# New figures in the account that orders TensorE's queue: weight loads behind a wait, transposes, projections, sums

## The chip, the core and the metric

The kernel runs on one core of one Trainium2 chip. The metric is the device time of one execution in microseconds, the median of three timed runs. The profile comes from one further execution of the same kernel. TensorE multiplies matrices and transposes, VectorE and ScalarE read its results out of eight banks, GpSimd works on data in the on-chip memory, and SyncE issues most of the DMAs.

## The reference, cut to what matters

One decoder layer is computed for 4 batches of 1,024 rows with 256 features: causal self-attention with 16 heads of 16, then cross-attention to 77 context rows under a mask, then a gated feed-forward part with 768 hidden features. Each part works on the layer-normalised rows and is added to the residual.

```python
x = x + attn(layernorm(x))      # scores = (gt*Qt K^T + (1-gt)*Q (M K)^T) * 16**-0.5, causal,
                                # softmax, times V, times Wo.T, plus bo
x = x + xattn(layernorm(x), ctx, ctx, mask)   # q Wq, k Wk, v Wv, softmax of 16 heads, times Wo
x = x + ffn(layernorm(x))       # h = silu(x wg.T / 127) * (x wu.T / 127);  h wd.T / 127
```

## The kernel before

The rows are cut into chunks of 512: two chunks n = 0, 1 for each of the four batches b. A chunk passes five generators, each of which emits its instructions piece by piece.

- `project` (two streams, one for each n) loads a chunk's rows, takes their statistics, normalises and transposes them, and makes q, k and v. A projection of q or k ends in `spread`: ScalarE writes the upper part `hi` (L782), VectorE the rest `lo` (L785, L787), and SyncE issues DMAs (L791) that lay both out by heads.
- `maxima` multiplies q with k in row blocks (L925, masks L933) and lets VectorE take each row's maximum `mt` (L938). After every second group of heads, `shift` transposes the maxima (L800) and leaves them as `ms` (L804).
- `attend` multiplies k with q (L998), adds the shift to the product on TensorE (L1004, masks L1011), lets ScalarE take the exponential `es` (L1017), and sums with the values (`weigh`, L1041). `quotients` transposes the sums back (L735) and divides; `out_proj` transposes (L197) and multiplies with the output weights (L769).
- `cross_attention` does the like for the 77 context rows (L1172 and L1180 for the maxima, L1226 for the scores, L1239 for the sums, L1146 for a mask).
- `ffn` normalises, transposes, multiplies with gate and up (`hidden`, L1296; ScalarE L1303 and L1308, VectorE L1304 and L1306, GpSimd L1309), and with the down weights (L1331, added to the rows at L1336).

Three further streams load and transpose the feed-forward weights, and one prepares the cross-attention weights.

The order of TensorE's queue is not written out; `weave` works it out while the program is built. Each stream offers its next piece: `piece(pe, use, at, free, mode, **take)`. `pe` is its length on TensorE, `use` a list of engines and lengths that come after it, `at` the time from which its data is expected, `take` the banks and buffers it needs. The mode is "rows" where the array's upper and lower halves work side by side (score products), "cols" where four strips of columns do (the sums), otherwise "whole". `weave` keeps the time at which TensorE's queue ends, the expected busy spans of ScalarE, VectorE, GpSimd and the DMAs, and the time at which each bank and buffer comes free. At every step it computes the start t of each offered piece, adds an offset from the table `LATES` (one row for a stream, one entry for each chunk of it), and takes the first in the list of streams whose sum is within 0.01 us of the least. A change of mode adds `SWITCH`, 0.11 us.

Where the account expects TensorE to be idle for more than 1.3 us and a bank is free, it fills in dummies: `stirred` issues int((idle - 0.7) / 0.235) matmuls (L93) ahead of the piece.

From the first moment until the second group of the first maxima, the weave's order holds for TensorE and VectorE. After that it holds for TensorE alone; the other engines' queues are ordered by the scheduler of the framework. The queues of all engines run in their order. The eight banks are shared: a "single" piece takes one, a "pair" two neighbouring ones.

```python
with tc.manual_schedule(engines={ENG.PE, ENG.DVE}):
    weave(*streams, until="begun")
tc.no_sync_barrier()
with tc.manual_schedule(engines={ENG.PE}):
    weave(*streams)
```

Of the kernel before, what the change touches and what calls it, by code (L numbers as in the profile page):

```python
# [27 lines left out]
def tile_decoder_layer(  # L28
# [126 lines left out]
    w4 = ctx.enter_context(tc.tile_pool(name="w4", bufs=6))  # L155
# [298 lines left out]
    LATE = 0.2  # L454
# [57 lines left out]
    def weave(*streams, until=None):  # L512
        while True:
# [4 lines left out]
            for s in live:  # L518
                p = s.next
                if p["cond"] is not None and not p["cond"]():  # L520
                    continue
                t = max(
                    tensor["end"], p["at"], *(slots[k].when(c) for k, c in p["take"].items()), 0.0
                )
                if p["pe"] and p["mode"] != tensor["mode"]:
                    t += SWITCH
                if p["use"] and p["take"]:

                    eng, us = p["use"][0]
                    t = max(t, busy[eng].start(t + p["pe"], us) - p["pe"] - 1.0)  # L530
                if t < 1.0e8:
                    can.append((t + (s.lates[s.chunk] if s.lates else 0.0), t, s))
# [221 lines left out]
    def out_proj(st, nat, t_nat, w, xt):  # L754

        yield piece(
            1.1, use=[("ACT", 1.05)], at=st.done + LATE, pair=1, w4=1, free=[t_nat]
        )
# [4 lines left out]
        for half in range(2):  # L763
            yield piece(2.0, at=at, use=[("DVE", 0.7)], free=t_aT * half, single=1)
            t = single().rearrange("p (i d) -> p i d", d=D)
# [40 lines left out]

    SPREAD = [("ACT", 0.62), ("DVE", 0.77), ("DMA", 8.0)]

# [24 lines left out]
    def project(st, b, n):  # L833
# [4 lines left out]
        else:  # L838
# [7 lines left out]
            scales = row_scales(xn)  # L846
            yield piece(0.0, use=[("DVE", 1.5)], at=st.done)
            normal_rows(xn, *scales)
            flags.add(("normal", b, n))
            yield piece(  # L850
                1.1, use=[("ACT", 1.05)], at=st.done + LATE, pair=1, w4=1, free=t_xn
            )
# [4 lines left out]
        for c in range(NC):  # L857
# [8 lines left out]
            if c == 0:  # L866
                for half in range(2):
                    yield piece(
                        2.0, use=[("ACT", 0.7)], single=1,
                        cond=lambda: (b, n) != (0, 0) or ("normal", 0, 1) in flags,  # L870
# [25 lines left out]
    def maxima(st, b, n):  # L896

        nk = n + 1
        for g in range(NG):
# [52 lines left out]
            if g % 2:  # L952
                yield piece(
                    0.55, use=[("ACT", 0.6), ("DVE", 0.77)], at=st.done + 0.6, single=1, f2=1,
                    ms=1,
                )
                ms = shift(mpad, "ms")
                st.release("single")
                st.release("f2")
                shifts[b, n, c] = ms, st.done + LATE, st.got["ms"][0]  # L960

    def attend(st, b, n):
# [6 lines left out]
        for g in range(NG):  # L969
# [9 lines left out]
            for kb in range(nk):  # L979
# [49 lines left out]
                def weigh(g=g, kb=kb, ki=ki, lo=lo, w=w, both=both, vs=vs, acc=acc, toks=toks,  # L1029
                          ready=ready):  # L1030
                    last = kb == nk - 1
                    yield piece(
                        0.03 + w * 1.77e-3, at=ready, free=toks, mode="cols",
                        use=[("ACT", 0.6)] if last else [],
# [35 lines left out]
    def quotients(st, tail, nat, t_nat):  # L1070
        rest, toks, at, g = tail
        yield piece(
            0.55, use=[("DVE", 0.75)], at=at, single=1, free=toks,
            **({"w4": 1} if nat is None else {}),
# [40 lines left out]
    def cross_attention(st, b, n):  # L1115
# [11 lines left out]
        scales = row_scales(xt, keep[:, it])  # L1127
        yield piece(0.0, use=[("DVE", 1.5)], at=st.done)
        xn = normal_rows(xt, *scales, wide([P, QT, D], "xn"))
        for j in range(2):  # L1130
# [3 lines left out]
        yield piece(  # L1134
            1.1, use=[("ACT", 1.05)], at=st.done + LATE, pair=1, w4=1, free=t_xn
        )
# [4 lines left out]

        yield piece(0.55, use=[("ACT", 0.6), ("DVE", 0.6)], single=1, mx=1)
        t_mB = st.got["mx"]
# [47 lines left out]
        for j in range(2):  # L1191
# [4 lines left out]
        yield piece(  # L1196
            0.55, use=[("ACT", 0.6), ("DVE", 0.77)], at=st.done + 0.8, single=1, f2=1, mx=1
        )
# [7 lines left out]
        for g in range(NG):  # L1206
            both, toks = [], []
            for p in range(2):
# [23 lines left out]
            yield piece(  # L1232
                0.95, use=[("ACT", 0.6)], at=st.done + LATE, free=toks, single=1, f2=1,
                mode="cols",
# [18 lines left out]
    def ffn(st, b, n, xt=None, rest=()):  # L1253
# [12 lines left out]
        if st:  # L1266
            xt, _ = xs[b, n]
            nc.sync.dma_start(x_dram[b, n], xt)
        scales = row_scales(xt)
        yield piece(0.0, use=[("DVE", 1.5)], at=done())  # L1270
        xn = normal_rows(xt, *scales, wide([P, QT, D], "xn"))
        yield piece(
            1.1, use=[("ACT", 1.05), ("DVE", 1.25)], at=done(), pair=1, w4=2, free=t_xn
        )
# [9 lines left out]
        def hidden(hc):  # L1284

            for k in range(2):
                yield piece(
                    0.95, at=at, single=1, free=t_x if k and hc == NH - 1 else [],
                    use=[("DVE", 0.7), ("ACT", 0.5), ("POOL", 1.3)] if k else
                    [("ACT", 0.6), ("DVE", 0.75)],  # L1290
# [19 lines left out]
            if st:  # L1310
                st.release("single", st.done - 2.2)
                give(t_h[0], st.done)
# [3 lines left out]
        for hc in range(NH):  # L1316
            held.append((yield from hidden(hc)))
            while len(held) == 3 or (hc == NH - 1 and held):
                now, held = held[:2], held[2:]
                at_h = max(h[3] for h in now)  # L1320
                for half in range(2):
                    yield piece(
                        1.2, at=at_h, use=[("DVE", 0.72)], single=1,
                        free=[t for h in now for t in h[2]] if half else [],
# [22 lines left out]
    def every(part, lates, chunks=range(NQ)):  # L1347
# [11 lines left out]
        [0.0000, 0.0000, 0.0000, 0.0000, 0.0000, 0.0000, -0.1816, 0.0000],  # L1359
        [0.0000, 0.0000, 0.0000, 0.0000, 0.0000, 0.0098, 0.0000, 0.0000],  # L1360
        [0.1824, 0.0000, 0.0000, 0.0465, 0.0104, 0.0000, 0.0000, 0.0000],
        [0.0212, -0.2908, 0.0000, 0.0000],
        [0.0391, 0.1944, 0.3468, 0.0000],
        [-0.3083, 0.0025, 0.0000, 0.0000, 0.4000, 0.3194, 0.3283, 10.7883],
    )
# [69 lines left out]
```

## Time and profile before

| | |
|---|---|
| time, median of 3 runs | 1212.08 us (1208.81 to 1214.08) |
| the profiled execution | 1210.99 us, span 1209.2 us |
| granted TensorE clock, mean | 0.979 |
| TensorE matmul busy | 1115.3 us, 92%, 9,147 instructions |
| TensorE weight load busy | 685.7 us, 57% |
| VectorE busy | 730.2 us, 60% |
| ScalarE busy | 559.6 us, 46% |
| GpSimd busy | 131.0 us, 11% |
| dummies (L93) | 88 matmuls, 24.0 us |

The weight loads (PEld) run beside the matmuls (PE) and are not to be added to them. Idle time of an engine stands with the work that ended it: "PEld banks L925 <- DVE mt L938" means that a weight load of line 925 waited until VectorE's `mt` of line 938 was done; the numbers are the total in us, how often, and the longest. In a line of the timeline the first number is the start, the second the length, both in us. In a line of a stretch the numbers after its length are busy time and instructions of PE, PEld, DVE, ACT and POOL, then the granted clock, the DMA share and GB/s. The matmuls' ends are modelled, so two starts are the safer measure of what a piece costs.

### The profile page before, as it was taken

The numbers are of one execution on the slowest core, as the hardware profiler recorded it, in microseconds if no ns is written. First come the engines' busy times: TensorE is split into PE (matmuls) and PEld (weight loads), VectorE is DVE, ScalarE is ACT, GpSimd is POOL, SyncE is SP. The second block draws the span as 40 slices with busy tenths as digits, with TensorE's granted clock in tenths as the row PEclk, the third lists the DMA queues.
The fourth block names the chain that finished last, engine by engine and source line by source line (L and its number), as shares of the span: only waits on it lengthen the run. The fifth ranks groups of instructions, "written<-read, shape, count | busy, mean of one in ns | idle before, by whom it ended". The sixth has DMA issues, their size and how long they took to land.

```text
span 1209.2 us, 22461 instructions
## 1 busy us (share of the span) xinstructions
PE 1115.3 (92%) x9147; PEld 685.7 (57%) x9147; DVE 730.2 (60%) x1287; ACT 559.6 (46%) x785; POOL 131.0 (11%) x138
## 2 busy tenths in 40 slices
PE   6898889899999999989899998999899999998997
PEld 4544445455665557546646556455456755556675
DVE  5678863254678776245758558632678893317544
ACT  3143346644444554744343553565244456663332
POOL 4030100001100002101200002010000101003112
PEclk9899999999999999989999999999899999999999
DMA  6992233147254206345362433109931204202300
GB/s 125 132 176 68 63 50 78 22 68 105 50 74 68 37 18 88 75 66 70 71 86 23 68 60 52 64 18 126 119 52 21 41 10 98 25 19 40 49 35 21
DMA packets 65441, 76.48 MB, mean 63 GB/s; under 512 B 22450, under 2 KB 39398, under 8 KB 65331
## 3 DMA queue, kind: packets, MB, share of 16 engines
q1 hardware_dynamic: 64227, 74.62, 39.2%
q8 instruction: 74, 1.21, 0.5%
q10 hardware_dynamic: 1104, 0.35, 0.1%
q14 instruction: 36, 0.29, 0.1%
HBM read 15.28 MB, written 9.33 MB: 20 GB/s over the span
## 4 chain that ended last, share of the span: by engine, by line
PE 67%; DVE 11%; DMA 11%; ACT 6%; issue 2%; POOL 2%; SPq 1%; ACTq 0%; DVEq 0%; POOLq 0%
PE banks L1041 10%; PE banks L998 7%; PE banks L925 6%; PE banks L1296 6%; PE banks L819 5%; PE banks L1004 4%; DMA q<-lo 4%; PE banks L769 4%; DVE mt L938 4%; PE banks L1226 4%; PE banks L1331 3%; DMA k<-lo 3%; ACT es L1017 3%; PE banks L1239 3%; PE banks L197 2%
## 5 line engine op out<-in xcount | busy, mean ns | idle before, releaser
L1017 ACT ACTIVATE es<-banks 128x1024 f32<-128x1024 f32 (+3 forms) x384 | 298.6, 811 | 243.6 <-PE banks L1011 162.5
L938 DVE TENSOR_REDUCE mt<-banks 128x2 f32<-128x1024 f32 (+3 forms) x384 | 349.8, 952 | 99.8 <-PE banks L933 65.8
L925 PE MATMUL banks<-k,q 64*128 64x512 f32 (+3 forms) x768 | 163.6, 427 | 27.5 <-DVE mt L938 15.8
L998 PE MATMUL banks<-q,k 64*128 64x512 f32 (+3 forms) x768 | 161.9, 414 | 18.0 <-DVE mt L938 5.9
L1041 PE MATMUL banks<-es,vs 128*32 128x512 f32 (+3 forms) x1536 | 167.1, 508 | 1.9 <-ACT aS L730 0.8
L925 PEld LDWEIGHTS banks<-k,q 64*128 64x128 f32 x768 | 75.2, 187 | 115.6 <-DVE mt L938 42.6
L1004 PE MATMUL banks<-ms,sel 64*128 64x512 f32 (+3 forms) x768 | 136.6, 348 | 2.2 <-DVE ms L804 2.2
L998 PEld LDWEIGHTS banks<-q,k 64*128 64x128 f32 x768 | 74.4, 188 | 98.4 <-ACT es L1017 36.5
L1309 POOL TENSOR_TENSOR hT<-h,hT 128x512 fp32r<-128x512 f32 x48 | 61.6, 1284 | 365.7 <-ACT hT L1308 365.7
L740 DVE RECIPROCAL rd<-banks 128x16 f32<-128x16 f32 x64 | 15.9, 252 | 107.2 <-PE banks L735 91.3
L1228 ACT ACTIVATE es<-banks 77x1024 f32<-77x1024 f32 x64 | 63.1, 1018 | 34.5 <-PE banks L1226 34.1
L1004 PEld LDWEIGHTS banks<-ms,sel 64*128 64x128 f32 x768 | 75.5, 190 | 5.9 <-DVE ms L804 2.5
L933 PE MATMUL banks<-cm_qk,id 64*128 64x128 bf16 (+1 forms) x1024 | 67.9, 211 | 0.0
L1303 ACT ACTIVATE h<-banks 128x512 f32<-128x512 f32 x48 | 28.7, 597 | 84.8 <-PE banks L1296 76.2
L1011 PE MATMUL banks<-cm_kq,id 64*128 64x64 bf16 (+1 forms) x1024 | 67.6, 210 | 0.0
L178 POOL TENSOR_TENSOR rs<-ve,mhalf 128x4 f32<-128x4 f32 x24 | 24.3, 1015 | 376.3 <-DVE ve L176 376.2
L1331 PE MATMUL banks<-wdT,hT 128*128 128x256 f32 x384 | 56.5, 294 | 3.1 <-POOL hT L1309 1.7
L1041 PEld LDWEIGHTS banks<-es,vs 128*32 128x32 f32 x1536 | 32.0, 109 | 41.7 <-issue 24.2
L1331 PEld LDWEIGHTS banks<-wdT,hT 128*128 128x128 f32 x384 | 49.7, 192 | 9.8 <-issue 3.3
L1186 DVE TENSOR_REDUCE mx<-banks 128x8 f32<-128x616 f32 x64 | 47.4, 791 | 12.6 <-PE banks L1180 12.5
L1304 DVE SCALAR_TENSOR_TENSOR h<-h,banks 128x512 f32<-128x512 f32 x48 | 32.9, 686 | 31.2 <-ACT h L1303 30.4
L730 ACT COPY aS<-banks 128x512 f32<-128x512 f32 x64 | 37.4, 588 | 28.8 <-PE banks L1239 21.8
(182 smaller groups left out, 1627.3 us busy)
## 6 DMA issues: line engine op xcount, KB each, us to landing
q<-hi SPq DMA_DIRECT2D x128, 128.0 KB, 6.3
q<-lo SPq DMA_DIRECT2D x128, 128.0 KB, 6.8
k<-hi SPq DMA_DIRECT2D x64, 128.0 KB, 4.9
k<-lo SPq DMA_DIRECT2D x64, 128.0 KB, 6.3
xr<-in_x_dram SPq DMA_DIRECT2D x8, 512.0 KB, 5.0
x<-in_x_dram SPq DMA_DIRECT2D x8, 512.0 KB, 5.7
x_dram<-x SPq DMA_DIRECT2D x8, 512.0 KB, 5.5
out_dram<-x SPq DMA_DIRECT2D x8, 512.0 KB, 2.9
```

What stands on the lines that cost most here:

```text
L925: nc.tensor.matmul(t[:, j, :w], q[r, a, i * P : (i + 1) * P], k[r, a, :w], start=True, stop=True,)
L933: nc.tensor.matmul(t[:, j, w - P + 64 * half : w], id2[r, half], cm_qk[r, half, 64 * half :], start=False, stop=True, skip_group_check=True,)
L938: nc.vector.tensor_reduce(mt[:, i, :, p, kc], t[:, :, :w], AX.X, ALU.max)
L998: nc.tensor.matmul(t[:, j, lo:], k[r, a, ki * P : (ki + 1) * P], q[r, a, lo:], start=True, stop=False,)
L1004: nc.tensor.matmul(t[:, j, lo:], sel[r, hp, :], ms[r, lo:], start=False, stop=True)
L1011: nc.tensor.matmul(t[:, j, lo : lo + 64 * (half + 1)], id2[r, half], cm_kq[r, half, : 64 * (half + 1)], start=False, stop=True, skip_group ...
L1017: nc.scalar.activation(es[:, :, lo:], t[:, :, lo:], AF.Exp)
L1041: nc.tensor.matmul(acc[0][W * jj : W * (jj + 1), lo:], vs[:, ki, V1 * h : V1 * h + W], both[jj // 2][:, jj % 2, lo:], start=(kb == 0), sto ...
L1228: nc.scalar.activation(es[:S2], t[:S2], AF.Exp)
L1296: nc.tensor.matmul(t, w[:, c, hc * P : (hc + 1) * P], v[:, c, :], start=(m == 0), stop=(m == len(terms) - 1),)
L1309: nc.gpsimd.tensor_tensor(hs[:, 1, :], h, hs[:, 0, :].bitcast(F32), ALU.subtract)
L1331: nc.tensor.matmul(t[:, i, :], h[1][:, v, m0 : m0 + P], w[:, h[0], :], start=(m == 0), stop=(m == len(terms) - 1),)
```

## The change

The rule for the start of a piece is split. A piece in another mode than the one before starts when its data, its banks and TensorE's queue are there, plus 0.11 us, as before. A piece in the same mode now starts 0.11 us after its data and banks are there, or at the end of the queue if that is later; the first weights of such a piece count as loaded behind the wait. Beside it some lengths are changed: on TensorE those of transposes, output and value projections, sums with the values, and the feed-forward part's down products; on the other engines those of the normalising, the spread, the value copy, the division and one copy of the hidden rows. The tables `LATES` have new entries. No computation is added, taken away or changed.

```diff
-                t = max(
-                    tensor["end"], p["at"], *(slots[k].when(c) for k, c in p["take"].items()), 0.0
-                )
-                if p["pe"] and p["mode"] != tensor["mode"]:
-                    t += SWITCH
+                t = max(p["at"], *(slots[k].when(c) for k, c in p["take"].items()), 0.0)
+                if p["pe"]:
+
+                    if p["mode"] != tensor["mode"]:
+                        t = max(t, tensor["end"]) + SWITCH
+                    else:
+                        t = max(t + SWITCH, tensor["end"])
+                t = max(t, tensor["end"])
...
-            1.1, use=[("ACT", 1.05)], at=st.done + LATE, pair=1, w4=1, free=[t_nat]
+            0.92, use=[("ACT", 1.05)], at=st.done + LATE, pair=1, w4=1, free=[t_nat]
...
-            yield piece(2.0, at=at, use=[("DVE", 0.7)], free=t_aT * half, single=1)
+            yield piece(1.75, at=at, use=[("DVE", 0.7)], free=t_aT * half, single=1)
...
-    SPREAD = [("ACT", 0.62), ("DVE", 0.77), ("DMA", 8.0)]
+    SPREAD = [("ACT", 0.69), ("DVE", 0.77), ("DMA", 8.0)]
...
-            yield piece(0.0, use=[("DVE", 1.5)], at=st.done)
+            yield piece(0.0, use=[("DVE", 1.9)], at=st.done)
...
-                        2.0, use=[("ACT", 0.7)], single=1,
+                        1.75, use=[("ACT", 0.6)], single=1,
...
-                        0.03 + w * 1.77e-3, at=ready, free=toks, mode="cols",
+                        0.03 + w * 1.68e-3, at=ready, free=toks, mode="cols",
...
-            0.55, use=[("DVE", 0.75)], at=at, single=1, free=toks,
+            0.46, use=[("DVE", 0.72)], at=at, single=1, free=toks,
...
-                0.95, use=[("ACT", 0.6)], at=st.done + LATE, free=toks, single=1, f2=1,
+                0.9, use=[("ACT", 0.6)], at=st.done + LATE, free=toks, single=1, f2=1,
...
-                    use=[("DVE", 0.7), ("ACT", 0.5), ("POOL", 1.3)] if k else
+                    use=[("DVE", 0.7), ("ACT", 0.62), ("POOL", 1.3)] if k else
...
-                st.release("single", st.done - 2.2)
+                st.release("single", st.done - 2.32)
...
-                        1.2, at=at_h, use=[("DVE", 0.72)], single=1,
+                        1.0, at=at_h, use=[("DVE", 0.72)], single=1,
...
-        [0.0000, 0.0000, 0.0000, 0.0000, 0.0000, 0.0098, 0.0000, 0.0000],
-        [0.1824, 0.0000, 0.0000, 0.0465, 0.0104, 0.0000, 0.0000, 0.0000],
-        [0.0212, -0.2908, 0.0000, 0.0000],
-        [0.0391, 0.1944, 0.3468, 0.0000],
-        [-0.3083, 0.0025, 0.0000, 0.0000, 0.4000, 0.3194, 0.3283, 10.7883],
+        [0.0000, 0.0000, 0.0000, 0.0000, 0.0000, 0.0000, 0.0000, 0.0000],
+        [0.1824, -0.0676, 0.0000, 0.0000, 0.0136, 0.0000, 0.0000, 0.0759],
+        [0.0000, 0.0000, 0.0000, 0.0000],
+        [0.1069, 0.1944, 0.3468, 0.0000],
+        [0.0000, 0.0000, -0.5736, 0.0000, 0.0000, 0.4883, 0.5315, -4.4614],
```

The same pairs of figures (1.1 to 0.92, 0.55 to 0.46, 1.5 to 1.9) are set at the other places where eight or four transposes or the normalising are offered: in `project`, `maxima`, `cross_attention` and `ffn`.

## The prediction

> **What bounds the kernel now.** I read the page first (busy shares and the forty slices), then the waits of TensorE and of its weight loads, then the timeline where a wait is seen at close range, then the groups of VectorE and ScalarE, and last the stretches of 20 and 100 us. The profiled execution took 1210.99 us, with a span of 1209.2 us; the median of the three timed runs is 1212.08 us, 1.1 us above it.
>
> ```profile
> PE 1115.3 (92%) x9147; PEld 685.7 (57%) x9147; DVE 730.2 (60%) x1287; ACT 559.6 (46%) x785; POOL 131.0 (11%) x138
> ```
>
> TensorE has work in 92% of the span and holds 67% of the chain that ended last. No other engine is above 60%. So the time is the length of TensorE's own queue plus what it loses between its pieces: 94 us shown as idle, and more that the rows hide, because a matmul whose weights are loaded late is shown as busy. Nothing in the change alters how much TensorE computes. What it can move is the losses.
>
> ```profile
> PEld banks L925 <- DVE mt L938: 42.6, 74, 3.9
> PEld banks L998 <- ACT es L1017: 36.5, 60, 1.2
> PEld banks L925 <- ACT es L1017: 29.0, 46, 1.2
> PEld banks L998 <- DVE mt L938: 12.3, 14, 3.8
> ...
> PE banks L925 <- DVE mt L938: 15.8, 26, 3.7
> ...
> PE banks L925 <- ACT es L1017: 6.9, 16, 0.8
> ```
>
> The first four lines are weight loads of the two score products (maxima L925, attention L998) that waited for a bank: 74+60+46+14 = 194 times. The last two are the same waits of L925 where TensorE's matmul side also stood visibly idle; with the two rows of L998 in that view (5.9 us, 3 times, and 5.1 us, 12 times) that makes 26+16+3+12 = 57 times and 33.7 us. So about 137 loads waited without a visible hole: the bank came free while the previous matmul was still draining. The old account calls those free. The next rows show they are not.
>
> ```profile
> 1177.74 0.19 PEld L1296 LDWEIGHTS banks<-xl,wgT 128*128 128x128 f32 x1 [0.47 <-DVE xl L1279]
> 1177.74 0.50 PE L1296 MATMUL banks<-xl,wgT 128*128 128x512 f32 x1
> 1177.85 0.19 PEld L1296 LDWEIGHTS banks<-xh,wgT 128*128 128x128 f32 x1
> 1178.08 0.39 PE L1296 MATMUL banks<-xh,wgT 128*128 128x512 f32 x1
> 1178.31 0.39 PE L1296 MATMUL banks<-xl,wgT 128*128 128x512 f32 x1
> ```
>
> The matmul whose load waited is 0.50 us long, its equals 0.39: the load's 0.11 us is added, and the next starts 0.34 us later and not 0.23. That is the price, and it is `SWITCH`.
>
> **The change, part by part.** It adds and removes no instruction by itself and adds no wait; it changes figures with which the order of TensorE's queue is worked out, so every term is an effect of another order.
>
> *Loading behind a wait.* Now a piece in the same mode that becomes ready at time r starts at r + 0.11 or at the queue's end, whichever is later; before, at r or the end. The order can thus prefer a piece that is long ready to one that arrives just now. At stake: 137 × 0.11 = 15.1 us; nothing at the other end, since the ready alternative is often in another mode, whose switch costs the same 0.11. Between these I take one in three avoided, about 46 × 0.11 = 5 us gained. That share is my choice, no row gives it.
>
> [...]
>
> *Lengths on TensorE.* The account takes off: eight-transposes 39 × 0.18 = 7.0 us; four-transposes 96 × 0.09 = 8.6; output and value projections 48 × 0.25 = 12.0; weighing, 16 × (1,280 + 3,328) columns × 0.00009 = 6.6; cross weighing 32 × 0.05 = 1.6; the FFN's down sums 48 × 0.2 = 9.6. Together 45 us. The rows support each:
>
> ```profile
> 439.60 1.09 PE L197 MATMUL banks<-ident,nat 128*128 128x128 f32 x8
> 440.62 1.06 PE L1041 MATMUL banks<-es,vs 128*32 128x512 f32 x8
> 441.62 0.66 PE L735 MATMUL banks<-ident,aS 128*128 128x128 f32 x4
> 442.12 0.60 PE L800 MATMUL banks<-ident,mpad 128*128 128x128 f32 x4
> 442.55 3.62 PE L769 MATMUL banks<-xwo,xnT 128*128 128x256 f32 x16
> ```
>
> From start to start: 1.02 (0.92 + 0.11 switch), 1.00 (0.89 + 0.11), 0.50 and 0.43 (0.46), 3.55 for two halves (1.75 each; the next piece starts at 446.10). The 45 us are none of the chip's time. They only move where the account expects the other engines to be ready, nearer to the truth. I take 1 us gained; between 6 us gained and 6 lost, the size of one stall of the kind described next.
>
> *Lengths elsewhere.* Normalising 1.5 to 1.9, ScalarE's spread 0.62 to 0.69, the hidden cast 0.5 to 0.62, the value copy 0.7 to 0.6: the groups by form give 4 × 459 ns = 1.84 us (L186), 687 ns (L782 with a bias), 617 ns (L1308) and 587 ns (L887). Most of it shifts expectations as above. One cost is certain, at the tail. The weave fills an expected idle time with dummies, (idle - 0.7) / 0.235 of them.
>
> ```profile
> 1168.22 5.86 PEld L93 LDWEIGHTS banks<-sel,selB 128*128 128x128 f32 x26
> ...
> 1171.66 1.38 DVE L186 TENSOR_SCALAR xn<-x,mv,rs 128x256 f32<-128x256 f32 x4 [1.12 <-POOL rs L178]
> ...
> 1174.35 1.03 PE L197 MATMUL banks<-ident,xn 128*128 128x128 f32 x8
> ```
>
> VectorE is done at 1173.04, but the transposes start at 1174.35: the dummies already overrun. With 0.4 us more expected idle there are 1 or 2 more, each 5.86 / 26 = 0.225 us: 0.5 us lost on the path, no cover there.
>
> *Tables.* An offset matters only where another stream competes. The FFN's last entry (10.7883 to -4.4614) works when every other stream has ended, so it is worth nothing. The other 14 changed entries move a stream's pieces by up to 0.6 us against the others; their worth is in the next term.
>
> *Stalls that another order redeals.*
>
> ```profile
> 860.00:880.00 20.00, 13.64 (x76) 7.31 (x78) 10.06 (x23) 7.12 (x10) 2.48 (x3) 0.74 0.71 95
> ...
> 900.00:1000.00 100.00, 96.65 (x869) 59.90 (x870) 88.19 (x127) 44.76 (x60) 7.62 (x7) 1.00 0.19 26
> ```
>
> In the first line TensorE loses 6.4 us. VectorE's queue is not ordered by the weave there: a `lo` (L785) waited in it for ScalarE's `hi`, that one for a spread DMA, and the shift `ms` (L804) stood behind, for which L1004 waited 2.2 us. The stretches 120:160, 520:540 and 600:620 lose another 7.0, 3.2 and 4.0 us. [...] A redeal can lose it or make another: from 12 us gained to 10 lost; I take 2 gained, because the account's errors (a spread on ScalarE at 0.62 where 687 ns are measured) sit just in that chain.
>
> Sum: 5 + 1 - 0.5 + 2 = 7.5 us gained: 1210.99 - 7.5 = 1203.5 for a profiled execution, 1204.6 by the median.
>
> **The rivals.** *Nothing to be had.* The just-arrived piece gives way only to one in another mode, which pays the same 0.11, or to one waiting for the same bank. Then the 194 waits stay about 194 and only the tail term and small redeals remain: 1212. For it: VectorE and ScalarE release the banks at their own pace (1.22 us for a wide maximum); against: three streams and more usually have something ready.
>
> *Slower: the maxima starve VectorE.* The pieces that wait most are the maxima (74 + 46 of the 194), so the new rule pushes these back, and VectorE's reduction starts later by as much. Place: the stretches with VectorE near full, above all 900:1000, busy 88.2 of 100. A later chunk has 64 maxima pieces; 64 × 0.11 = 7 us of pushed-back reductions, against 11.8 us of slack. Once pushes pass 11.8 us in such a stretch (each set aside about twice), the shift comes late, attention's L1004 waits for `ms` as at 868, and TensorE runs dry: some 4 us and 2 us of half clock in perhaps two of the four batches, 12 us in all: 1224. For it: the margin is thin; against: where nothing else is ready the maximum still goes first.
>
> *The change does not do what it says.* The figures agree with the rows, so this is only that a truer account need not give a better order; it lies within the two rivals.
>
> **How the numbers follow.** Faster by order and account 0.42, own range 1192 to 1206; nothing to be had 0.22; slower by starving or a worse redeal 0.36, own range 1218 to 1230. The likeliest is 1204.6. Cases of both signs hold most of the chance, so the range runs from 1192 to 1226: gains at both bounds of the first two terms at one end, the starved batches at the other. The bound of 0.5% (6 us, about what a measurement of this kernel can tell from no change) is at 1206 and 1218; the chances are those of the cases.
>
> **What would show it.** Right: fewer than 160 waits of the weight loads in the four lines shown, TensorE's idle time below 90 us, the stretch around 860 without a half clock, and 27 or 28 dummies before the last transposes. Wrong: the four lines as before (no gain), or more PE waits on `ms` (L804) and VectorE's busy share in the fullest hundred us below 85% (starving), or a new stretch with a clock under 0.8.

## The result: slower by 0.7%, and the profile after

| | before | after |
|---|---|---|
| median of ten runs each, same chip visits | 1212.8 us (1208.15 to 1215.59) | 1220.85 us (1215.35 to 1226.38) |
| the profiled execution | 1210.99 us, span 1209.2 | 1220.41 us, span 1218.6 |
| granted TensorE clock, mean | 0.979 | 0.968 |
| TensorE idle (span less PE busy) | 93.9 us | 91.6 us |
| dummies (L93) | 88 | 112 |
| last reduction of the maxima (`mt`) ends at | 1000.3 us | 1040.1 us |

The ratio after to before is 1.0070, 95% interval 1.0045 to 1.0095: slower, where 1204.6 us was forecast. The lines of the changed kernel stand 3 higher (L925 is now L928, L998 L1001, L938 L941, L1017 L1020).

First the busy line of the page, then the group of L93 (the dummies), and then one line of the forty slices, the granted clock, after and before:

```profile
PE 1127.0 (92%) x9171; PEld 699.8 (57%) x9171; DVE 727.3 (60%) x1287; ACT 558.0 (46%) x785; POOL 131.0 (11%) x138
```

```profile
L93 PE MATMUL banks<-sel,selB 128*128 128x512 f32 x112 | 31.7, 431 | 6.4 <-DVE selB L590 6.4
```

```profile
PEclk9799999999899899998999998999989999999999
```

```profile
PEclk9899999999999999989999999999899999999999
```

Over the whole span TensorE is not idler than before. It is busy 11.7 us longer, with 24 instructions more; these are the dummies, 7.7 us of it. The rest, 4.0 us, is the same matmuls taking longer: six slices have an 8 or less in the clock's row, where three had before. A matmul at half clock shows as busy (before, the projection L819 x4 at 873.52, at a clock of 0.50, is 3.78 us long, where the one at 858.58 is 1.88), so this loss is found in no list of waits.

The waits of the weight loads, as the prediction read them (total us, times, longest us):

```profile
PEld banks L928 <- DVE mt L941: 47.0, 69, 3.6
PEld banks L1001 <- ACT es L1020: 45.9, 70, 1.4
PEld banks L928 <- ACT es L1020: 36.6, 55, 1.6
...
PEld banks L1001 <- DVE mt L941: 12.1, 14, 2.3
```

69 + 70 + 55 + 14 = 208, where there were 194. With the 57 that also left the matmul side idle taken off, 151 waited without a visible hole, where 137 had. The rule that charges 0.11 us for a load behind a wait has not made such loads rarer. The matmul side:

```profile
PE banks L928 <- DVE mt L941: 20.3, 24, 3.2
PE banks L928 <- ACT es L1020: 8.5, 18, 1.4
PE banks L329 <- DMA wk_n<-in_L_attn_Wk_dram: 8.1, 1, 8.1
PE banks L93 <- DVE selB L590: 6.4, 1, 6.4
```

The wait of L928 for `mt` grew from 15.8 to 20.3 us at about the same number, that for `selB` at the start from 2.4 to 6.4 (five dummies, which need `selB`, now go ahead of the second chunk's transposes). Other holes shrank by as much.

Where the time goes is found by laying the two traces side by side at equal amounts of TensorE work done (an estimate, as each matmul counts with what its kind usually takes). At about 926 us the changed kernel is some 1 us ahead; at about 1148 us it is some 10 us behind. The net loss arises in that stretch. Two lines from the stretches of 100 us after, and the second of them before:

```profile
900.00:1000.00 100.00, 92.10 (x845) 56.50 (x846) 71.88 (x115) 43.95 (x61) 5.85 (x5) 0.97 0.23 42
1000.00:1100.00 100.00, 97.32 (x873) 53.76 (x871) 40.24 (x66) 63.28 (x84) 1.86 (x2) 1.00 0.18 28
```

```profile
1000.00:1100.00 100.00, 99.44 (x837) 60.05 (x838) 32.27 (x77) 62.20 (x84) 7.66 (x7) 1.00 0.23 43
```

Before, the first of these had TensorE at 96.65 and VectorE at 88.19; now VectorE is at 71.88 and the maxima it has not done come 40 us later. Over these 200 us TensorE is idle for 10.6 us, where it was for 3.9. By then the fifth feed-forward chunk (b = 2, n = 0), which before lasted until 1008 us beside those maxima, is used up: it ended at 909 us. The stretch of the prediction's starved batch is the right one. That TensorE lacks the chunk's work there is a reading of these lines and is not shown.

A stall at close range, from the timeline (start, length; in brackets the idle time before it and what ended it):

```profile
408.62 1.02 POOL L178 TENSOR_TENSOR rs<-ve,mhalf 128x4 f32<-128x4 f32 x1 [42.37 <-DVE ve L176]
...
409.95 1.38 DVE L186 TENSOR_SCALAR xn<-x,mv,rs 128x256 f32<-128x256 f32 x4 [1.41 <-POOL rs L180]
...
411.24 3.02 DVE L941 TENSOR_REDUCE mt<-banks 128x2 f32<-128x1024 f32 x4
...
412.52 0.33 PE L928 MATMUL banks<-k,q 64*128 64x128 f32 x2 [3.21 <-DVE mt L941]
```

VectorE's queue reaches a normalising whose `rs` GpSimd has not yet made. VectorE stands 1.41 us, the normalising itself takes 1.38 us more, the reductions behind it are late, they hold the banks, and TensorE stands 3.21 us. The weave had not put the normalising there: in this part VectorE's queue is ordered by the framework. The half clock that follows (L772 x16 in 6.34 us, where it takes 3.6) lasts 6.8 us.

### The profile page after: what moved, and what is told of

It reads as the page before. It is cut to its first block, busy times and chain, and to the rows that moved or that the text cites. A ratio compares the mean times of both kernels' runs of the same rounds, so it can differ in the third digit from the quotient of the medians.

```text
span 1218.6 us, 22516 instructions
## 1 busy us (share of the span) xinstructions
PE 1127.0 (92%) x9171; PEld 699.8 (57%) x9171; DVE 727.3 (60%) x1287; ACT 558.0 (46%) x785; POOL 131.0 (11%) x138
## 4 chain that ended last, share of the span: by engine, by line
PE 70%; DVE 13%; ACT 6%; DMA 4%; issue 4%; POOL 2%; SPq 1%; ACTq 0%; DVEq 0%; POOLq 0%
PE banks L1044 11%; PE banks L928 7%; PE banks L1001 7%; PE banks L822 6%; PE banks L1299 5%; DVE mt L941 5%; PE banks L772 5%; PE banks L1007 4%; PE banks L1229 3%; PE banks L1334 3%; ACT es L1020 3%; PE banks L197 2%; PE banks L738 2%; PE banks L1242 2%; PE banks L1014 2%
## 5 line engine op out<-in xcount | busy, mean ns | idle before, releaser
L941 DVE TENSOR_REDUCE mt<-banks 128x2 f32<-128x1024 f32 (+3 forms) x384 | 351.6, 954 | 123.3 <-PE banks L936 92.6
L1020 ACT ACTIVATE es<-banks 128x1024 f32<-128x1024 f32 (+3 forms) x384 | 298.2, 811 | 238.5 <-PE banks L1014 160.9
L928 PE MATMUL banks<-k,q 64*128 64x512 f32 (+3 forms) x768 | 164.7, 433 | 33.9 <-DVE mt L941 20.3
L1001 PE MATMUL banks<-q,k 64*128 64x512 f32 (+3 forms) x768 | 161.1, 414 | 11.0 <-DVE mt L941 4.2
L1044 PE MATMUL banks<-es,vs 128*32 128x512 f32 (+3 forms) x1536 | 164.6, 502 | 1.4 <-ACT es L1020 0.8
L928 PEld LDWEIGHTS banks<-k,q 64*128 64x128 f32 x768 | 76.8, 193 | 121.4 <-DVE mt L941 47.0
L1001 PEld LDWEIGHTS banks<-q,k 64*128 64x128 f32 x768 | 73.8, 188 | 97.8 <-ACT es L1020 45.9
L1334 PEld LDWEIGHTS banks<-wdT,hT 128*128 128x128 f32 x384 | 52.8, 205 | 7.3 <-POOL hT L1312 1.9
L205 ACT COPY xnT<-banks 128x1024 f32<-128x1024 f32 x32 | 32.3, 1013 | 47.3 <-PE banks L197 47.2
```

Of the source, the lines that this page charges most:

```text
L928: nc.tensor.matmul(t[:, j, :w], q[r, a, i * P : (i + 1) * P], k[r, a, :w], start=True, stop=True,)
L941: nc.vector.tensor_reduce(mt[:, i, :, p, kc], t[:, :, :w], AX.X, ALU.max)
L1001: nc.tensor.matmul(t[:, j, lo:], k[r, a, ki * P : (ki + 1) * P], q[r, a, lo:], start=True, stop=False,)
L1020: nc.scalar.activation(es[:, :, lo:], t[:, :, lo:], AF.Exp)
L1044: nc.tensor.matmul(acc[0][W * jj : W * (jj + 1), lo:], vs[:, ki, V1 * h : V1 * h + W], both[jj // 2][:, jj % 2, lo:], start=(kb == 0), sto ...
L1334: nc.tensor.matmul(t[:, i, :], h[1][:, v, m0 : m0 + P], w[:, h[0], :], start=(m == 0), stop=(m == len(terms) - 1),)
```

## The experiments

In the weave's account the end of TensorE's queue is a number that falls out when the program is built; "the account's end" below is that. "Searched" tables are tables `LATES` found by changing entries and keeping what brings this end down. Ratios are to the kernel before in the same chip visit, with their 95% interval. The letters of the theories are those of the expectations.

**Is it the order or the figures?** The weave's choices (1,644 steps) are written out from one kernel and used in the other; the figures then still set the dummies and which bank a piece takes.

```diff
-                _, t, s = next(c for c in can if c[0] <= soon)
+                want = streams[ORDER.pop(0)]
+                _, t, s = next(c for c in can if c[2] is want)
```

Order of before with the new figures and rule:

> The changed kernel's rule, lengths and bank choice, but the streams are taken in exactly the order of the kernel before (1,644 pieces, written out). Theory 1, the order is the loss: about 1213 us, at most 2 us more for dummies (the account then plans 105 of them and not 88, 17 x 0.225 = 3.8 us, most of it in idle time). Theory 2, the new figures cost by themselves, through more dummies and other banks: 1218 us or more.

Order of after with the old figures and rule:

> The kernel before's rule, lengths and bank choice, with the streams taken in exactly the order of the changed kernel. Theory 1, the order is the loss: about 1219 us (94 dummies and not 112, up to 2 us less than the changed kernel). Theory 2, the figures cost by themselves: about 1213 us.

Measured: 1216.81 us, ratio 1.0022 (1.0004 to 1.0040), and 1223.62 us, 1.0079 (1.0049 to 1.0108). The order makes the loss with the old figures too. The new figures on the old order cost 0.2%, between the two theories, beside 17 dummies more (105), 17 × 0.225 = 3.8 us at most.

**Does the account's end say anything of the chip?** The kernel before with all entries of `LATES` at zero; its account's end is 53.7 us later.

> The kernel before with every entry of LATES at zero. The account reckons the end of TensorE's queue 53.7 us later than with its tables (1221.3 against 1167.6 us, as the weave leaves it while the program is built). If a gain in the account is a gain on the chip, 1255 to 1270 us; if the tables mostly fit the account's own errors, 1215 to 1235 us.

Measured: 1268.53 us, 1.0456 (1.0408 to 1.0503), 55 us more by the medians. A large difference in the account arrives on the chip in full. The changed kernel is the other case: its own account has its order 15.0 us shorter than the old one (1158.6 to 1143.6), the old account has it 6.4 longer (1167.6 to 1174.0), and the chip 8 to 10 longer. Here two accounts are compared, and an order tuned in one with an order tuned in the other.

**Other tables under the same figures.** The changed kernel and the kernel before, each with tables searched again.

```diff
-        [0.1824, -0.0676, 0.0000, 0.0000, 0.0136, 0.0000, 0.0000, 0.0759],
+        [0.0000, 0.0224, 0.0048, 0.0084, 0.0000, 0.0000, -0.0126, 0.0427],
...
```

> The changed kernel with other tables, found by a search from zero for the least end of the queue in its own account (1139.9 us by the account, 3.7 us less than with its own tables). Theory 3, the new account is the worse guide: about 1220 us like the changed kernel, 1217 to 1224. Theory 4, each order is one draw among many near-equal ones and the changed kernel drew badly: anywhere from 1205 to 1225, and more likely below 1220.

> The kernel before (old rule, old lengths) with other tables, found by a search from zero in its own account (end of the queue 1166.4 us by the account, 1.2 us less than with its own tables). Here the fifth feed-forward chunk is planned at 767 to 802, before the last maxima chunk (869 to 964). Theory F (filler): work for TensorE must be left for the last maxima; it is spent too early here, so 1218 to 1223 us. Theory L (the old account is the better ruler): 1210 to 1214 us. Theory D (every order is a draw within some 8 us): anything from 1208 to 1222.

Measured: 1219.76 us, 1.0052 (1.0031 to 1.0073), and 1208.97 us, 0.9969 (0.9941 to 0.9997). The first cannot part theories 3 and 4, as both forecast such a time. The theory that the early fifth feed-forward chunk costs the time (F) missed here: it is early in the second of these too, and that one is faster.

**Rule or lengths?** The new rule with the old lengths, and the new lengths with the old rule, each with searched tables; then the order of the second of these with rule and lengths both.

> The kernel before with the new rule for a load behind a wait alone, old lengths, and tables searched anew for this account. The fifth feed-forward chunk is planned at 829 to 976, across the last maxima (857 to 991). If the rule does the harm: 1218 to 1224 us. Theory F: no worse than before, 1208 to 1215 us. Theory L (the lengths do the harm): 1210 to 1217 us, since the old account reckons this order 4.1 us longer than that of before.

> The changed kernel with the old rule for the start of a piece, so the new lengths alone, and tables searched anew for this account. The fifth feed-forward chunk is planned at 815 to 944, across the last maxima (817 to 946). If correcting the lengths does the harm: 1217 to 1225 us. Theory F: 1207 to 1214 us. The old account reckons this order 8.2 us shorter than that of before: by it, 1205 us.

> The changed kernel's rule, lengths and bank choice, with the streams taken in exactly the order of the lengths-only kernel that took 0.978 of before. If the order is everything: 1185 to 1191 us (110 dummies and not 106). If the rule for a load behind a wait costs by its dummies and banks: 1195 us or more.

Measured: 1208.20 us, 0.9968 (0.9949 to 0.9987); 1186.37 us, 0.9782 (0.9751 to 0.9813); 1185.54 us, 0.9771 (0.9748 to 0.9795). Neither half of the change does harm by itself where tables are searched for it, and the rule costs nothing on an order where it had no say. The rule with the old lengths comes out as the old figures with searched tables did (0.9969), so the gain of 0.3% is not shown to be the rule's. The cores view and the clock row of the lengths alone:

```profile
core 0: 1184.0 us, clock 0.983
```

```profile
PEclk9799999999999999999999999999999999999999
```

**The changed kernel's tables searched further, and the feed-forward chunk held back.** The first starts the search at the tables of the change; the second also lets the fifth feed-forward chunk begin only when the last chunk is projected.

```diff
+            and ((b, n) != (2, 0) or ("projected", 3, 1, 0) in flags)
```

> The changed kernel with nothing but its tables searched on from where they stand (end of the queue by its own account 1132.7 us and not 1143.6). The fifth feed-forward chunk stays early (746 to 833, the last maxima 833 to 960), as in the changed kernel. Theory T (the changed tables were simply left at a poor place): 1205 to 1214 us, some 11 us less than the changed kernel. Theory F (filler spent too early): still 1217 or more. Theory R (the new rule makes the account a bad guide): 1216 to 1224 us.

> The changed kernel where the fifth feed-forward chunk may not begin before the last batch's second chunk is projected, and tables searched for that (1129.2 us by its account; the chunk is planned at 857 to 949, the last maxima at 815 to 951). Theory F: 1195 to 1206 us, clearly below the kernel searched on without the hold. Theory T: about the same as that one, within 5 us (its account differs by 3.5 us).

Measured: 1214.84 us, 1.0012 (0.9991 to 1.0033), and 1203.76 us, 0.9927 (0.9904 to 0.9950). The first lies just above the range of theory T, the second in that of theory F. The kernel with the hold is 11 us faster by the medians, but it has tables of its own too, and other tables alone move the time by more (below), so this does not show the cause. The order of after with the chunk's pieces alone moved was not tried.

**Score products at the length they have.** By the figures of the expectation the account is short by 0.06 to 0.08 us for a score piece of attention and by 0.04 to 0.06 us for one of the maxima. With 384 pieces of each that is some 40 to 50 us, an estimate.

```diff
-                            0.02 + w * 4.1e-4 + (0.11 if kc == n else 0.0), mode="rows", pair=1,
+                            0.07 + w * 4.1e-4 + (0.11 if kc == n else 0.0), mode="rows", pair=1,
...
-                        0.04 + w * 8.2e-4 + (0.11 if diag else 0.0), mode="rows", pair=1, es=1,
+                        0.12 + w * 8.2e-4 + (0.11 if diag else 0.0), mode="rows", pair=1, es=1,
```

> The changed kernel with longer score products in the account (maxima 0.07 + and not 0.02 +, attention 0.12 + and not 0.04 +, by what the two traces show above the account: 0.04 to 0.06 us for each maxima piece, 0.06 to 0.08 for each attention piece), and tables searched for it. Its account ends at 1165.7 us, near the chip's own. Theory S (the change only shortened what was too long, and what was too short now misleads): 1185 to 1200 us. Theory T: between 1200 and 1215, since the old account reckons this order at 1172.1, no better than that of before.

Measured, with tables searched: 1197.38 us, 0.9878 (0.9852 to 0.9904). That is what theory S forecast, 1.9% under the changed kernel, with the fifth feed-forward chunk still early. Since a fresh search by itself moves the time by as much (below), the lengths are not shown to be the cause.

**Two stalls by hand.** The order of after with four pieces moved ahead of the stalls at 413 and 750 us.

> The changed kernel with its own order written out, and four of its 1,644 pieces moved: the two cross-attention output products that followed the stall at 412.5 us stand before it, and the two down products that followed the stall at 751.4 us stand before that. In the changed kernel's profile TensorE waits there 3.2 and 1.65 us for maxima of VectorE, whose queue was held by a normalising that waited for GpSimd (409) and by mask writes (749), and each is followed by 6.8 us at half clock. If stalls of this kind and the half clock after them are the loss: 3.5 + 3.4 at the first and 1.2 + 3.4 at the second, 11.5 us in all, so 1208 to 1213 us. If only the idle time counts: 1216 us. If later waits take it back: 1219 to 1222 us.

Measured: 1216.96 us, 1.0041 (1.0012 to 1.0071), some 3.5 us less than the changed kernel by the ratios, of the 11.5 expected. It is the 1216 us of the second theory by number, but not for its reason, since only one stall went, that at 750. The other only moved, as the timeline shows (one line higher, L773 is the output product):

```profile
413.49 2.76 PE L773 MATMUL banks<-xwo,xnT 128*128 128x256 f32 x7 [3.20 <-DVE mt L942]
```

The product that was to fill the hole needed a bank that VectorE's late reduction held. There TensorE's order alone did not mend what VectorE's order broke.

**VectorE's queue in the weave's order to the end.** One word is added; on both kernels, and then on the lengths alone.

```diff
-    with tc.manual_schedule(engines={ENG.PE}):
+    with tc.manual_schedule(engines={ENG.PE, ENG.DVE}):
```

> The changed kernel where VectorE's queue too keeps the order of the weave to the end, instead of the framework's order. If maxima held behind a normalising that waits for GpSimd are what the account does not see: fewer waits of L928 for mt, less half clock, 1200 to 1212 us. If the weave's own order holds VectorE as often, at a piece that waits for ScalarE (lo behind hi, ms behind mh): 1220 to 1245 us.

> The kernel before, changed only so that VectorE's queue too keeps the weave's order to the end. If the framework's order of VectorE is a loss of both kernels alike: 0.98 of before, about 1189 us, and still 0.7% below the changed kernel so treated (0.9873). If it is what makes the difference between the two: about 0.987 to 0.995, so that the two treated kernels are within 0.7% of each other or in the other order.

> The lengths-only kernel with its searched tables (0.978 of before), and VectorE's queue kept in the weave's order to the end. If the two gains add: 0.96 of before, 1163 to 1170 us. If its order had already avoided the stalls behind VectorE's queue (38 us of idle time behind VectorE against 48 in the changed kernel): 1180 to 1190 us.

Measured: changed kernel 1197.09 us, 0.9873 (0.9831 to 0.9914); kernel before 1179.46 us, 0.9751 (0.9729 to 0.9773); lengths alone 1164.74 us, 0.9619 (0.9601 to 0.9637). The first two came out below their forecasts; the third is where the two gains add up. The framework's order of VectorE's queue costs all three about 2% (1.7 to 2.5%), so it does not tell the changed kernel from the one before: with it gone the ratio of the two is 0.9873 / 0.9751 = 1.0125. The row of waits for `mt` in the kernel before with the queue woven, and its clock:

```profile
PE banks L925 <- DVE mt L938: 10.9, 23, 1.2
```

```profile
core 0: 1177.2 us, clock 0.984
```

The longest of these waits fell from 3.7 to 1.2 us. In the changed kernel so treated it fell from 3.2 to 2.4 us.

**Tables good in several accounts; further searches.** Tables searched for the mean end of four accounts, with the lengths and the woven queue of the kernel just shown; a second search for the lengths alone; and another for the full change.

> As the kernel before this one in the list, with tables searched for the least mean end over four accounts (old, new, lengths only, longer scores): by them 2.4 us less on average in the three that it was not searched in before, 1.6 us more in its own. If the accounts' errors are what a search gains by: 1 to 6 us below that kernel. If every order is a draw: within 6 us on either side.

> The lengths-only kernel (old rule) with tables of a second search, from zero; it ends at 1133.9 us in its own account, where the first ended at 1121.1, and at 1168.2 us in the old account (before: 1167.6). If the corrected lengths are what made the first 2.2% faster: 1190 to 1200 us. If what counts is that the first order is short in every account: about before, 1207 to 1217 us.

> The changed kernel, all its figures and its rule, with tables of another search; the order is short in every account (its own 1125.6, 18.0 us less than with the changed tables; old account 1153.2, 14.4 us less than before). If the new rule or the lengths make the account a bad guide as such: 1205 us or more. If the change was slower only because of the place at which its tables were left: 1180 to 1195 us.

Measured: 1164.61 us, 0.9609 (0.9594 to 0.9625), no different from the tables of a single account; 1193.50 us, 0.9849 (0.9825 to 0.9873); 1189.37 us, 0.9822 (0.9797 to 0.9848). The last is the changed kernel with nothing but other tables, and it is 1.8% faster than the kernel before. Both of the last two lie in the range of the theory that clears the figures: the change was slower because of the place at which its tables were left.

All searches side by side:

| figures in the account | ratios of the orders found |
|---|---|
| old rule, old lengths | 1 (before), 0.9969 |
| new rule, old lengths | 0.9968 |
| old rule, new lengths | 0.9782, 0.9849 |
| new rule, new lengths | 1.0070 (after), 1.0052, 1.0012, 0.9822 |

Within the last row the tables alone move the time by 2.5%, as much as most differences between rows. Within this row the account did rank the orders searched in it: ends of 1143.6, 1139.9, 1132.7 and 1125.6 us took 1220.85, 1219.76, 1214.84 and 1189.37 us. Orders found elsewhere fall out of line. By the same figures the order of before ends at 1158.6 us and took 1216.81, and the order of the lengths alone ends at 1132.9 and took 1185.54, some 29 us less than the one that ends at 1132.7. The two fast orders with the new lengths under the old rule suggest that the lengths help; two searches do not prove it.

## Why the prediction was wrong

**Which step failed.** It failed at what an order is worth, in two terms.

*Loading behind a wait*, 5 us gained: nothing of it is seen. The "one in three avoided" was a choice without a row, and the count went from 194 to 208. The price of 0.11 us stands (0.50 us against 0.39); that the order would avoid such loads did not come. Late loads and switches as a whole did not answer to the rule either: by matching each piece with its matmuls and the shortest of its kind, an estimate, they fell from 162.7 to 154.9 us, but in the old figures with fresh tables (0.9969) they fell to 155.3 as well. A load that did not wait had no such price in the rows of before: all of them use 128 rows, the load at 1177.85 runs inside the matmul of 1177.74, and the starts at 1178.08 and 1178.31 are 0.23 us apart.

*Stalls that another order redeals*, 2 us gained out of a band of 12 gained to 10 lost: this is the term that decided, and it came out at the lost end: the order of after costs 10 us with the old figures (1.0079) and some 6 with the new (1.0070 against 1.0022). The reason given, that the account's errors sit in that chain, was the wrong kind of argument. The stall at 860 did go, as forecast, and the stretch 860:880 now reads

```profile
860.00:880.00 20.00, 19.66 (x115) 13.71 (x114) 11.86 (x28) 9.01 (x13) 2.74 (x4) 1.00 1.08 131
```

but half clock came close behind it (880:900 has a clock of 0.91) and at 413, 751 and 901 us instead. A truer figure makes a truer sum for a given order; which order is taken is set by the tables, and these were left 18 us above an end that a later search found with the same figures (1143.6 and 1125.6). VectorE's real queue is not in the account, and half clock only as 5 us of it after a hole of more than 1.3 us that no dummies fill; both are redrawn with each order. Moving all entries by 0.01 us at random moves the account's own end by some 20 to 90 us, so no small edit is small here.

**The other terms.** *The tail*: 28 dummies ahead of the last transposes, as forecast.

```profile
1177.27 6.33 PEld L93 LDWEIGHTS banks<-sel,selB 128*128 128x128 f32 x28
...
1180.70 1.39 DVE L186 TENSOR_SCALAR xn<-x,mv,rs 128x256 f32<-128x256 f32 x4 [1.12 <-POOL rs L178]
...
1183.86 1.04 PE L197 MATMUL banks<-ident,xn 128*128 128x128 f32 x8
```

VectorE is done at 1182.09 and the transposes start 1.8 us later, where it was 1.3: the 0.5 us of the prediction, rightly sized. But dummies grew elsewhere too, 24 in all, 24 × 0.225 = 5.4 us, of which only a part fills holes that would have been there. *Lengths*, 1 us gained: 0.2% lost with the order held (the first experiment), inside the band of 6 either way. *The clock*: the prediction has no row for the 2 us of half clock that its slower rival counts for a stall, nor for the band of 12 gained to 10 lost, which is a choice. In the trace of before the four matmuls of L819 at 873.52 took 3.78 us instead of 1.88, 1.9 us more; with the 6.4 us that TensorE lost in 860:880 that stall cost 8.3 us, an estimate. How many half-clock stretches the new order would have, the prediction did not ask. Half-clock time in the profile rose from 51.4 us in 10 periods to 78.7 us in 14.

**How the loss divides.** By the same matching of pieces, before to after: visible idle 78.2 to 75.6 us, dummies 22.5 to 29.8, excess at half clock 21.4 to 34.3, late loads and switches 162.7 to 154.9. That is -2.6 + 7.3 + 12.9 - 7.8 = 9.8 us, against 9.4 us of span. Over the whole span the loss stands under half clock and dummies, but where it arises it does not. Up to 926 us the half clock (9.4 us more) and the dummies (3.8) were paid for by less idle time (7.7) and fewer late loads and switches (6.5). Of the 10 us lost from there to 1148 us, 4.8 are idle time, 2.6 dummies, 2.1 late loads and switches, and 0.7 half clock (estimates: for each matmul, the time to the next start against the mean of its kind at full clock). No one item is the loss: the changed kernel with its tables searched further has a clock of 0.965 in its profile, some 85 us at half clock by 2 × (1 - clock) × span, more than the 78.7 here, and takes 6 us less.

**The signs.** Fewer than 160 waits: 208. Idle below 90 us: 91.6. Neither sign of a gain came. VectorE's share in the fullest hundred below 85%: the stretch 900:1000 fell from 88.19 to 71.88, and the fullest is now 600:700 with 73.57: the sign of the *starving* rival, and its own range, 1218 to 1230, holds the result. A new stretch with a clock under 0.8 came too: 20:40 and 40:60 stand at 0.74 each, where both had 0.83. The mechanism of the rival was only half met: the maxima did come later and TensorE is idler there, but its wait for `ms` is a single one of 0.3 us, where before it was one of 2.2:

```profile
PE banks L1007 <- DVE ms L807: 0.3, 1, 0.3
```

```profile
PE banks L1004 <- DVE ms L804: 2.2, 1, 2.2
```

That its range holds the result is thus in part luck. That the change itself need not be at fault, the rival folded into the others, is what the experiments show: the same figures with other tables give 0.9822.

**What stays open.** Which single decision makes the changed order lose some 10 us between 926 and 1148 us. Using up the fifth feed-forward chunk early is a candidate that three faster orders speak against as a rule: there it ends at 841, 829 and 818 us, and they reach 0.9969, 0.9878 and 0.9849.

## What to carry to other kernels

Where a planner's order is tuned in its own account, a gain smaller than the account's errors (here 15 us, between orders tuned in two accounts, against score products that are some 40 to 50 us short) said nothing of the chip, while one of 54 us arrived in full. Within one account the searched orders came in the order of their ends, but two orders with equal ends were 29 us apart. So after a change of figures, search the tables again, measure several orders and keep the best, and judge the figures by the group. First look for what the account does not hold at all: here one engine's queue that it did not order was worth 1.7 to 2.5%, by one word. And compare the clock's row before the waits: here half clock, 78.7 us of it against 51.4, made matmuls longer that show as busy, and that is in no list of waits.

## What the runs showed of the hardware

**Half clock went with most of the spread between runs of one kernel.** In the two traces, before and after, the granted clock is either 1 or 0.5. Over 112 runs of the kernel before, with half-clock time worked out as 2 × (1 - clock) × span, the mean is 61.3 us and the time followed it with a correlation of 0.91 and a slope of 0.34 us for each us. A run of 1206.13 us had a clock of 0.980, one of 1216.91 had 0.968. Ten runs of the changed kernel have 75.6 us and the same slope; if it holds between the two kernels, the 14.3 us more answer for 14.3 × 0.34 = 4.9 of the 8 us, an estimate. It is no rule between kernels: the changed kernel with tables searched anew has a mean clock of 0.976, the kernel before 0.974 beside it, and takes 0.5% longer. One of the two fastest kernels has 0.990 in its profile:

```profile
core 0: 1163.5 us, clock 0.990
```

**Half clock came in portions, on one grid in each of the two traces.** Its 24 periods, 10 before and 14 after, are 3.4, 6.8 or 10.2 us long, but for the last of each trace, which runs past the span's end; within each trace all of them start on one grid of 3.413 us, to within 0.002. Cut into these windows (from 100 us on), a window at full clock in which TensorE was busy for less than half by the profile was followed by half clock 12 times out of 12 (two of them behind TensorE's last matmul), one between 0.5 and 0.7 in 8 of 23, one above 0.7 in none of 588. Ahead of the other 18 of these 20 periods the longest hole was under 3.3 us 15 times, with a median of 1.8. The window ahead of the half clock at 412.9 us was busy for 0.11 of its time, nearly all of the hole of 3.21 us lying in it; the one ahead of that at 867.6 us in the kernel before, with a hole of 2.2 us, for 0.45; the one ahead of that at 245.6 us in the changed kernel, with holes of 0.62 and 0.57 us, for 0.65. So in these traces short holes in one window were followed by half clock as a long one was.

**A wait in VectorE's queue grew on its way to TensorE.** In the stall at 408 to 413 us, 1.41 us of VectorE waiting for GpSimd, with the 1.38 us of the work it waited to do, became 3.21 us of TensorE waiting for a bank, and then 6.8 us at half clock, in which the sixteen matmuls of one product took 6.34 us, where the sixteen at 442.55 us before took 3.62.
